# Scaling and adding a tile's first two gathered slots later, their product in fourth place, and row shifts of a weight one iteration later

## The chip, the core and the metric

The kernel runs on one core of one Trainium2 chip. The metric is the device time in microseconds (us). Before the change three runs gave 629.84, 631.80 and 633.22 us; the median is 631.8. A profile was taken of one more execution, and all times of single instructions come from it.

## What is computed

The inputs are x, 4096 rows of 512 numbers, and a 4096 x 4096 adjacency matrix with few nonzero entries in a row besides the diagonal. Two layers follow each other. The first is a graph convolution with a residual and a normalisation; the second is graph attention with a residual and a normalisation.

```python
a = adj + eye; d = sum(a, axis=1) ** -0.5
out = relu((d[:, None] * a * d[None, :] @ x) @ W.T + b)
x = layernorm(x + out)
...
scores = scores + 0.01 * eye - 1e16 * (1.0 - maximum(adj, eye))
x = layernorm(x + einsum('hqm,hmk,hko->qo', softmax(scores), v, Wo))
```

Entries of the adjacency matrix are below 1, so the mask term of -1e16 times (1 - adj) leaves the attention of each row on its own diagonal, where adj is replaced by at least 1. The attention of a row is then its own value vector, and the second layer is one product with a combined weight of Wv and Wo. The kernel uses this, and it tests at the end whether it may. Should the test fail, a general version (the function general) runs after it; with these inputs it does not.

## The kernel before

**Tiles.** The rows are cut into 32 tiles of 128 (NT = 32). The function few_edges_below_one does the work in two phases.

**First phase** (lines 1063 to 1108, about the first 217 us of the profile). Its loop runs over t from 0 to 32. In each iteration a tile of adj is loaded (a_t, kept for scanning, or a_n, which only passes through to be summed), ACT sums its rows or tests for negative entries (L710, L715), and for some tile j the product y = d * (x W^T) is made: rows of x turned by PE (L689), copied by ACT (L694), multiplied (L703), scaled by ACT (L736) and written to DRAM by POOL's queue. Between these steps a generator, second_weights (L617), builds the combined weight wvo: transposes ("t" steps), products ("p" steps), and at its end the step sums and centre. A "p" step begins on PE in one iteration and its end is called in the next through the variable left (L1090). The function centre takes the mean out of the weight's rows on DVE (L654), makes four row numbers (L658), and adds them to the weight on ACT (L660), four instructions in a row.

**Scanning.** DVE finds the entries of each row: for each of 8 segments of a tile it takes the 8 largest values and their places (L752, L753), then merges and sorts them in short instructions (L774, L783, L780). The generator steps holds this work and some(n) emits the next pieces of it, a fixed share in each step of either phase. match then moves the slots of a tile between rows in six stages, named KEY, ACROSS, RANKS, PERM, MOVE and END: a key made by ACT (L848), its transpose on PE (L855), ranks on ACT (L862), a permutation on DVE (L872), matmuls on PE (L881, L884), and copies and sums on DVE (L892 to L895). The result is, for every tile, nine slots: column numbers (cols_all) and weights (wr_all).

**Second phase** (lines 1112 to 1396). The loop runs over tiles i in an order of its own, and inside over steps k from 0 to 8. For each slot POOL gathers the 128 rows of y that it names, 256 KB, by an indirect DMA (gather, L1119), 18 slots ahead of use, into a pool of 19 buffers. ACT builds a 128 x 128 matrix for each slot (spread, L999), and PE multiplies matrix and gathered rows and adds up in zs[i] (L1337). Each product is two matmul instructions in the profile.

**Slots added ahead.** Some slots of a tile share one matrix. The list summed (L1116) says how many: 1 for tile 0, 2 for tiles 1 to 22, 5 (SAME) for tiles 23 to 31. presum(i, 0) scales the first slot on ACT in place (L1141); presum(i, k) adds a further slot times its weight on DVE (L1143). One product then serves them all; it uses matrix KH and slot 0. In the kernel before, presum of tile i+1 is called at the last steps of tile i: for two slots at k = 7 and k = 8. The product of the sum is the first of a tile (k = 0), and the other slots follow at k = 2 to 8.

**After the products.** One step into the next tile, scaled (L1194) and residual (L1202) on DVE make the first layer's row sums; PE turns the rows (L689) and multiplies them by wvo (L703); ACT and DVE normalise, and ACT's queue writes the result. load_own(i+2) at k = 2 loads two tiles through SP's queue (L1134, L550); reload (L993) loads tiles of adj again for scanning, through the same queue.

**What sets the order.** The instructions are emitted in program order, and a scheduler of the framework orders those of each engine by priority and by when it reckons them ready; keep_in_program_order pins an instruction. The framework also hands out the buffers and sets the semaphores. Each engine works its instructions off in the order so fixed.

Of the kernel before, what the change touches and what calls it, by code (L numbers as in the profile page):

```python
# [419 lines left out]
def few_edges_below_one(  # L420
# [18 lines left out]
    nc = tc.nc  # L439
    N, D = x.shape  # L440
    H, _, KD = wks.shape
    NT = N // P
# [10 lines left out]
    KH = 9  # L453
# [107 lines left out]
    def load_first(t, parts=1):  # L561
        if t in early or t in resident:
            return load_a(t, parts=2 if t == NT - 1 else parts)
        return load_a(t, pn, "a_n")
# [23 lines left out]
    def split_b():  # L588

        t = [p1.tile([P, D], FP, name="x_t", bufs=6)[:3] for _ in range(3)]  # L590
        nc.gpsimd.dma_start(t[0], bcast_rows(b0, D)[:3])
        for n in range(2):
            nc.vector.tensor_tensor(t[n + 1], t[n], t[n].bitcast(BF)[:, 1::2], ALU.subtract)
        for n in range(3):
            u, e = t[n].bitcast(BF)[:, 1::2], ident[:3, n : n + 1]
            if n == 0:
                nc.vector.tensor_scalar(b3, u, e, None, op0=ALU.mult)
            else:
                nc.vector.scalar_tensor_tensor(b3, u, e, b3, op0=ALU.mult, op1=ALU.add)

    def load_second_weights():

        nc.sync.dma_start(
            wv.rearrange("p (h f) -> p h f", h=H),
            wvs.rearrange("h (p j) k -> p h (j k)", j=ND),
        )
        su1 = p1.tile([P, 2, ND, D], FP, name="wo", bufs=1)
        nc.sync.dma_start(su1[:, 0], wo.rearrange("(r a) k o -> (a k) r o", a=2))
        return su1

    def order_second_weights():
        nc.gpsimd.tensor_copy(
            w_nat.rearrange("p j (h k) -> p j h k", h=H),
            wv.rearrange("p (h j k) -> p j h k", h=H, j=ND),
        )

    def second_weights(su1):  # L617

        wo_sb, wvT = su1[:, 0], su1[:, 1]

        def transposed(r):
            pt = ps_t.tile([P, 512], FP, name="pt")
            for j in range(ND):
                nc.tensor.transpose(pt[:, ts(j, P)], w_nat[:, j, ts(r, P)], ident)
            return pt

        def put(r, pt):
            nc.scalar.copy(
                wvT[:, r, :].rearrange("q (p j) -> q j p", j=ND),
                pt[:, :D].rearrange("q (j p) -> q j p", j=ND),  # L630
            )

        def product(dc):
            pa = ps_a.tile([P, D], FP, name="acc")
            for r in range(NP):
                nc.tensor.matmul(
                    pa, wvT[:, r, ts(dc, P)], wo_sb[:, r, :], start=(r == 0), stop=(r == NP - 1)
                )
            return pa

        def add(dc, pa):
            nc.scalar.copy(wvo[:, dc, :], pa)
            nc.gpsimd.tensor_tensor(wvo[:, dc, ts(dc, P)], wvo[:, dc, ts(dc, P)], ident, ALU.add)

        def sums():
            pa = ps_a.tile([P, D], FP, name="acc")
            for dc in range(ND):
                nc.tensor.matmul(pa, ones, wvo[:, dc, :], start=(dc == 0), stop=(dc == ND - 1))
            return pa

        def centre(pa):
            row = const.tile([P, ND], FP, name="row")
            for dc in range(ND):
                nc.vector.scalar_tensor_tensor(  # L654
                    wvo[:, dc, :], pa, -1.0 / D, wvo[:, dc, :], op0=ALU.mult, op1=ALU.add,
                    accum_out=row[:, dc : dc + 1],
                )
            nc.vector.tensor_scalar(row, row, -1.0 / D, None, op0=ALU.mult)  # L658
            for dc in range(ND):
                nc.scalar.activation(  # L660
                    wvo[:, dc, :], wvo[:, dc, :], AF.Identity, bias=row[:, dc : dc + 1]
                )

        for r in range(NP):
            yield "t", (lambda r=r: transposed(r)), (lambda pt, r=r: put(r, pt))
        for dc in range(ND):
            yield "p", (lambda dc=dc: product(dc)), (lambda pa, dc=dc: add(dc, pa))
        yield "p", sums, centre

    def load_keys():  # L670
        su2 = setup_tile()
        for n, w in ((0, wqs), (1, wks)):
            nc.sync.dma_start(
                su2[:, n].rearrange("p c d -> p (c d)"),
                w.rearrange("h (a d) k -> (h a) (d k)", a=P // H),
            )
        return su2
# [307 lines left out]
    def some(upto):  # L985
        while count[0] < upto:
            count[0] += 1
            next(work, None)
# [38 lines left out]
    def projected(t):  # L1027

        return t + 1 + sum(t >= e for e in SOONER)
# [30 lines left out]
        a_tiles[t] = load_first(t)  # L1060
    transpose_w()
    split_b()
    setup, left = iter(()), None
    for t in range(NT + 1):
        if t == 0:
            su1 = load_second_weights()
        if t + DEEP < NT:
            a_tiles[t + DEEP] = load_first(t + DEEP)
        if t == 3:
            order_second_weights()  # L1070
            setup = second_weights(su1)

        ahead = sum(at <= projected(t) for at, _ in due)
        turn = sum(at <= projected(t + (t >= LEAD)) for at, _ in due)
        turn_rows(turn, 3)
        kind, begin, end = next(setup, (None,) * 3) if ahead - done[1] < 2 else (None,) * 3
        got = begin() if kind == "t" else None
        if t < NT:
            if t in early:
                sum_negative(t, a_tiles[t])  # L1080
            else:
                sum_rows(deg_all[:, t : t + 1], a_tiles[t][:, : N // 2 if t == NT - 1 else N])
                more = None
                if t == NT - 1:
                    more = small.tile([P, 1], FP, name="more")
                    sum_rows(more, a_tiles[t][:, N // 2 :])
                scaling(t, more)
            if t in again:
                del a_tiles[t]
        if left:  # L1090
            left()
            left = None
        for j in [j for at, j in due if at == t]:
            keep_y(j, us.pop(j))
        while done[1] < ahead:
            j = due[done[1]][1]
            us[j] = times(evacuate(p1, "xT", turned.pop(j), t >= NT - 7), wT)
            done[1] += 1
        turn_rows(turn, 2)
        if kind == "t":  # L1100
            end(got)
        if kind == "p":
            left = lambda end=end, pa=begin(): end(pa)
        if t < NT - 5:
            match(*ALL)
        some((t + 1) * RATE)
# [6 lines left out]
    p2 = ctx.enter_context(tc.tile_pool(name="second", bufs=2))  # L1113
    AHEAD = 18

    summed = [1] + [2] * (NT - 1 - 9) + [SAME] * 9  # L1116
    slots = {}

# [18 lines left out]
    def presum(i, k):  # L1137
        g = slots[i * KH]
        w = wr_all[:, order[i], 1, k : k + 1]
        if k == 0:  # L1140
            nc.scalar.activation(g, g, AF.Copy, scale=w)  # L1141
            return
        nc.vector.scalar_tensor_tensor(  # L1143
            g, slots.pop(i * KH + k), w, g, op0=ALU.mult, op1=ALU.add
        )

    def last_products(ks, c):

# [128 lines left out]
    yo, zs, hs, pts, hTs, ws, sts, mats, halves = ({} for _ in range(9))  # L1277
# [28 lines left out]
    for i in range(NT + 2):  # L1306
# [6 lines left out]
        for k in range(KH):  # L1313
# [7 lines left out]
            if i == NT - 1:  # L1321

                if k == 4:
                    last_products((0, *range(SAME, KH)), HALVES[0])
                if k == 6:
                    scaled(i, HALVES[0])
                    residual(i, HALVES[0])
                    bias(i, HALVES[1])
                    last_products((0, *range(SAME, KH)), HALVES[1])
                if k == 7:  # L1330
                    pts[i] = transpose_rows(hs[i], (0, 1))
                    hTs[i] = p2.tile([P, ND, P], FP, name="hT", bufs=2)
                    tc.keep_in_program_order(nc.scalar.copy(
                        hTs[i][:, 0:2].rearrange("p c s -> p (c s)"), pts[i][:, : 2 * P]
                    ))
            elif i < NT and not 0 < k < summed[i]:
                nc.tensor.matmul(  # L1337
                    zs[i], mats[i][:, KH if k < summed[i] > 1 else k, :], slots.pop(i * KH + k),
                    start=False, stop=(k == KH - 1),
                )  # L1340
            if i < NT:
                gather(i * KH + k + AHEAD)
            build(1)
            if i + 1 < NT and k >= KH - summed[i + 1] and summed[i + 1] > 1:
                presum(i + 1, k - (KH - summed[i + 1]))
            if k == 1 and has_p and not ends:
                scaled(p)
# [74 lines left out]
```

## Time and profile before

| what | value |
|---|---|
| median of three runs | 631.8 us (629.84 to 633.22) |
| profiled execution, its own time | 632.17 us |
| its span, first to last instruction | 630.3 us |
| mean granted clock of PE | 0.946 |
| busy: PE, DVE, ACT, POOL | 523.2, 555.0, 497.7, 357.6 us |
| DMA, mean over the span | 345 GB/s |
| gathers on POOL | 288, 0.996 us each |
| products of the second phase (L1337) | 450 matmul instructions, 0.626 us each |
| additions of slots on DVE (L1143) | 58, 0.741 us each |
| scalings of slots on ACT (L1141) | 31, 0.713 us each |

Busy time counts an engine's instructions from start to end. Matmuls are pipelined, and their ends are modelled, so two matmuls that are listed with 0.6 us each may start 0.43 us apart. A wait in a listing stands in brackets after the instruction that waited, with its length and what ended it. "<-DVE g L1143" means that the engine was idle until DVE's instruction of line 1143, which writes tile g, had ended.

### The profile page before, as it was taken

To read this page: it belongs to the slowest core of one execution; us is meant where nothing else is said; L and a number is where in the kernel's file an instruction comes from. 1 tells how busy PE (TensorE), PEld (TensorE's weight loads), DVE (VectorE), ACT (ScalarE), POOL (GpSimd) and SP (SyncE) were. 2 spreads that over 40 slices of the span, in tenths; PEclk is the share of its full clock that TensorE was granted. 3 is DMA by queue.
4 is the path that set the end of the run, shared out by engine and by line. 5 is a ranking of instruction groups with operands and counts; after the bars stand their busy time and mean duration, and the time that the engine had idled before them with its cause. 6 is when DMAs were issued, how large, how long until landed. Compare 5 with 4: busy or idle time off the path is not lost. (4 is left out here: it accounts for less than half of the span.)

```text
span 630.3 us, 7782 instructions
## 1 busy us (share of the span) xinstructions
PE 523.2 (83%) x1537; PEld 241.2 (38%) x1537; DVE 555.0 (88%) x2037; ACT 497.7 (79%) x1093; POOL 357.6 (57%) x465
## 2 busy tenths in 40 slices
PE   1599886699968052799897999999999999989793
PEld 1344333345423021344443444444444444433251
DVE  5699999999999998799998999999999999854441
ACT  0859668688899858479978988998989899877751
POOL 5232323233323277677775667777777777777740
PEclk9999988999999566799998999999999999989898
DMA  8999999899999587999999999999999988888851
GB/s 327 401 420 423 421 427 428 332 416 426 425 425 424 238 282 226 354 383 397 398 397 399 402 368 327 389 354 381 313 394 366 317 265 280 280 276 244 286 163 38
DMA packets 57273, 217.68 MB, mean 345 GB/s; under 512 B 8701, under 2 KB 9981, under 8 KB 52864
## 3 DMA queue, kind: packets, MB, share of 16 engines
q1 hardware_dynamic: 23888, 115.48, 46.1%
q0 software_dynamic: 28192, 92.30, 41.7%
q10 hardware_dynamic: 5136, 9.31, 4.0%
q14 instruction: 43, 0.35, 0.2%
q8 instruction: 14, 0.23, 0.1%
HBM read 200.28 MB, written 16.78 MB: 344 GB/s over the span
## 5 line engine op out<-in xcount | busy, mean ns | idle before, releaser
L1124 POOL DMA_INDIRECT g<-y,cols_all x288 | 286.9, 996 | 101.9 <-issue 46.6
L1337 PE MATMUL acc<-g,s_t 128*128 128x512 f32 x450 | 221.6, 626 | 38.4 <-DVE g L1143 22.2
L752 DVE MAX8 v_all<-a_t 128x8 f32<-128x512 f32 x256 | 166.7, 678 | 15.9 <-DMA a_t<-in_adj_dram 15.9
L753 DVE FIND_INDEX8 idx<-v_all,a_t 128x8 uint32<-128x512 f32 x256 | 173.2, 684 | 0.0
L703 PE MATMUL acc<-wT,xT 128*128 128x512 f32 x256 | 121.8, 625 | 20.6 <-ACT xT L694 19.8
L1337 PEld LDWEIGHTS acc<-g,s_t 128*128 128x128 f32 x450 | 84.2, 199 | 133.0 <-issue 101.0
L703 PE MATMUL acc<-wvo,hT 128*128 128x512 f32 x256 | 117.8, 602 | 5.2 <-ACT hT L694 4.2
L715 ACT ACTIVATE dump<-a_t 128x2048 uint8<-128x2048 f32 (+1 forms) x50 | 119.2, 2383 | 0.0
L703 PEld LDWEIGHTS acc<-wT,xT 128*128 128x128 f32 x256 | 49.2, 200 | 78.1 <-issue 53.1
L703 PEld LDWEIGHTS acc<-wvo,hT 128*128 128x128 f32 x256 | 48.8, 193 | 66.9 <-issue 57.0
L1006 ACT ACTIVATE sq<-cols,wr_all 128x128 f32<-128x128 f32 x160 | 58.8, 393 | 6.7 <-DMA a_t<-in_adj_dram 6.1
L1143 DVE SCALAR_TENSOR_TENSOR g<-g,wr_all 128x512 f32<-128x512 f32 x58 | 43.0, 741 | 23.4 <-ACT s_t L1016 6.6
L1010 ACT ACTIVATE s_t<-sq,wr_all 128x128 f32<-128x128 f32 x128 | 58.5, 485 | 0.2
L722 POOL TENSOR_SCALAR deg<-deg_all 128x1 f32<-128x1 f32 x32 | 7.3, 229 | 78.5 <-DVE deg_all L970 45.5
L710 ACT ACTIVATE dump<-a_n 128x4096 uint8<-128x4096 f32 x13 | 47.3, 3639 | 0.0
L550 POOL DMA_DIRECT2D x_t<-in_x_dram x32 | 18.0, 565 | 41.6 <-PE pt L689 35.4
L783 DVE MAX8 top<-key 128x8 f32<-128x64 f32 x192 | 36.2, 213 | 0.1
L1141 ACT ACTIVATE g<-g,wr_all 128x512 f32<-128x512 f32 x31 | 22.1, 713 | 16.4 <-issue 10.0
L694 ACT COPY hT<-pt 128x512 f32<-128x512 f32 x31 | 18.0, 579 | 18.1 <-PE pt L689 17.9
L774 DVE SCALAR_TENSOR_TENSOR key<-key,top 128x64 f32<-128x64 f32 x128 | 32.2, 272 | 0.0
L694 ACT COPY xT<-pt 128x512 f32<-128x512 f32 x32 | 18.9, 600 | 14.3 <-PE pt L689 12.4
L1194 DVE SCALAR_TENSOR_TENSOR h<-yo,own_all,acc 128x512 f32<-128x512 f32 (+1 forms) x33 | 23.7, 719 | 5.1 <-PE acc L1337 2.6
(135 smaller groups left out, 661.4 us busy)
## 6 DMA issues: line engine op xcount, KB each, us to landing
a_t<-in_adj_dram SPq DMA_DIRECT2D x17, 2048.0 KB, 21.5
a_t<-in_adj_dram SPq DMA_DIRECT2D x56, 512.0 KB, 12.4
a_n<-in_adj_dram SPq DMA_DIRECT2D x13, 2048.0 KB, 15.8
x_t<-in_x_dram POOLq DMA_DIRECT2D x32, 256.0 KB, 11.3
yo<-y SPq DMA_DIRECT2D x32, 256.0 KB, 6.5
x_t<-in_x_dram SPq DMA_DIRECT2D x32, 256.0 KB, 7.3
out_dram<-r_t ACTq DMA_DIRECT2D x31, 256.0 KB, 6.1
y<-y_t POOLq DMA_DIRECT2D x18, 256.0 KB, 14.7
```

The lines of the kernel that those rows point to most:

```text
L694: copy = nc.scalar.copy(dst.rearrange("p c s -> p (c s)"), pt[:, :D])
L703: nc.tensor.matmul(u, srcT[:, dc, :], w[:, dc, :], start=(dc == 0), stop=(dc == ND - 1))
L710: nc.scalar.activation(dump[:, : part.shape[1]], part, AF.Copy, accum_out=dst)
L715: nc.scalar.activation(dump[:, o], a_t[:, o], AF.Relu, scale=-1.0, accum_out=neg_all[:, t, halves[0] : halves[0] + 1],)
L752: long.append(lambda o=o, seg=seg: nc.vector.max(v[:, o], seg))
L753: long.append(lambda o=o, seg=seg: nc.vector.max_index(idx[:, o], v[:, o], seg))
L783: return lambda: nc.vector.max(top[:, f, r * 8 : r * 8 + 8], keyf[:, f])
L1006: nc.scalar.activation(sq, cols1, AF.Square, bias=wr[:, 2, k : k + 1])
L1010: nc.scalar.activation(s_t[:, k, :], away(), AF.Relu, scale=wr[:, 3, k : k + 1], bias=wr[:, 1, k : k + 1],)
L1124: nc.gpsimd.indirect_dma_start(out=slots[j], out_offset=None, in_=y[:, :], in_offset=bass.IndirectOffsetOnAxis(ap=cols_all[:, t, k : k + 1 ...
L1143: nc.vector.scalar_tensor_tensor(g, slots.pop(i * KH + k), w, g, op0=ALU.mult, op1=ALU.add)
L1337: nc.tensor.matmul(zs[i], mats[i][:, KH if k < summed[i] > 1 else k, :], slots.pop(i * KH + k), start=False, stop=(k == KH - 1),)
```

## The change

Two things are moved. First, the four row shifts on ACT become a step of their own, of a kind "s", that the generator yields after "p" of sums. It has nothing to begin on PE, and its end, shift, is called at the left() of the iteration after centre's or a later one. The four instructions are pinned to program order. The variable row carries the four numbers from centre to shift.

Second, for tiles with two summed slots (1 to 22), the scaling on ACT is called at k = 8 of the tile before, not 7, and the addition on DVE at k = 1 of the tile itself, not at k = 8 of the one before. PE's products run in the order slot 2, 3, 4, then the sum at k = 3 (BASE), then slots 5, 6, 7, 8 at k = 4 to 7; k = 8 has none. Tile 0 and the tiles with five summed slots keep their order.

```diff
@@ second_weights
             nc.vector.tensor_scalar(row, row, -1.0 / D, None, op0=ALU.mult)
+            return row
+
+        def shift(row):
             for dc in range(ND):
-                nc.scalar.activation(
+                tc.keep_in_program_order(nc.scalar.activation(
                     wvo[:, dc, :], wvo[:, dc, :], AF.Identity, bias=row[:, dc : dc + 1]
-                )
+                ))
...
         yield "p", sums, centre
+        yield "s", None, shift
@@ loop of the first phase
-        if left:
-            left()
-            left = None
+        row = (left() if left else None) or row
+        left = None
...
+        if kind == "s":
+            left = lambda end=end, row=row: end(row)
@@ second phase
+    BASE = 3
...
+    def product(i, m, j, stop):
+
+        nc.tensor.matmul(zs[i], mats[i][:, m, :], slots.pop(j), start=False, stop=stop)
...
+            elif i < NT and summed[i] == 2:
+                if k == BASE:
+                    product(i, KH, i * KH, False)
+                else:
+                    m = k + 2 if k < BASE else k + 1
+                    if m < KH:
+                        product(i, m, i * KH + m, m == KH - 1)
             elif i < NT and not 0 < k < summed[i]:
-                nc.tensor.matmul(
-                    zs[i], mats[i][:, KH if k < summed[i] > 1 else k, :], slots.pop(i * KH + k),
-                    start=False, stop=(k == KH - 1),
-                )
+                product(i, KH if k < summed[i] > 1 else k, i * KH + k, k == KH - 1)
             if i < NT:
                 gather(i * KH + k + AHEAD)
             build(1)
-            if i + 1 < NT and k >= KH - summed[i + 1] and summed[i + 1] > 1:
+            if i + 1 < NT and summed[i + 1] == 2 and k == KH - 1:
+                presum(i + 1, 0)
+            if i < NT and summed[i] == 2 and k == 1:
+                presum(i, 1)
+            if i + 1 < NT and k >= KH - summed[i + 1] and summed[i + 1] > 2:
                 presum(i + 1, k - (KH - summed[i + 1]))
```

More of the change, by code (lines that the diff above doesn't have):

```diff
@@ L1062, in few_edges_below_one @@
     split_b()
-    setup, left = iter(()), None
+    setup, left, row = iter(()), None, None
     for t in range(NT + 1):
```

## The prediction

> **What bounds the kernel now.** I read the busy shares by slice first, then the waits, then the timelines of single engines. In the slices a digit 9 means 90% or more of 15.76 us.
>
> ```profile
> PE   1599886699968052799897999999999999989793
> ...
> DVE  5699999999999998799998999999999999854441
> ACT  0859668688899858479978988998989899877751
> ...
> PEclk9999988999999566799998999999999999989898
> DMA  8999999899999587999999999999999988888851
> ```
>
> DVE (VectorE) stands at 9 from the third slice to the thirty-fourth, but for three of them. The table by stage says the same in numbers:
>
> ```profile
> 390.00:540.00 150.00, 149.91 (x463) 67.98 (x462) 149.89 (x610) 137.96 (x404) 114.37 (x114) 1.00 0.95 336
> 540.00:606.00 66.00, 58.30 (x157) 25.07 (x156) 35.45 (x105) 48.87 (x138) 50.77 (x51) 0.95 0.85 271
> ```
>
> The columns are length, PE, weight load, DVE, ACT, POOL. From 390 to 540 us PE and DVE are both full. After 540 DVE has run out of scanning, and no engine is full. I then asked the timeline of DVE for its idle time between 30 us and the end of scanning (about 548 us). There are seven gaps above 0.3 us: 0.62 at 129.96 (ended by PE), 7.55 at 256.67, 0.47 at 276.41 (PE), 0.42 at 293.21 (ACT), 0.67 at 333.81 (ACT), 1.67 at 347.01 (PE) and 0.32 at 386.91 (its own result). That is 11.7 of 518 us. **VectorE's fixed work is the bound until 548 us**; whatever frees another engine counts only as far as it closes one of these gaps. The largest is seen here:
>
> ```profile
> 256.67 1.29 DVE L752 MAX8 v_all<-a_t 128x8 f32<-128x512 f32 x2 [7.55 <-DMA a_t<-in_adj_dram]
> ```
> ```profile
> 222.26 0.43 SPq L550 DMA_DIRECT2D x_t<-in_x_dram  x1
> 247.58 0.33 SPq L1134 DMA_DIRECT2D yo<-y  x1
> 248.85 0.33 SPq L550 DMA_DIRECT2D x_t<-in_x_dram  x1
> 249.23 4.16 SPq L545 DMA_DIRECT2D a_t<-in_adj_dram  x5
> ```
>
> The first reload of adjacency rows sits in SP's queue behind load_own(3), whose buffers come free with tile 0's scaled and residual on DVE (246.80 and 248.13). DVE starves on a load that DVE itself released late.
>
> PE's waits, the target of the edit:
>
> ```profile
> PE acc L1337 <- DVE g L1143: 22.2, 8, 11.0
> ```
> ```profile
> 248.27 10.18 PE L1337 MATMUL acc<-g,s_t 128*128 128x512 f32 x16 [10.96 <-DVE g L1143]
> ...
> 263.13 5.29 PE L1337 MATMUL acc<-g,s_t 128*128 128x512 f32 x6 [4.14 <-DVE g L1143]
> ```
>
> The eight waits are 10.96, 4.14 (tiles 1, 2), 1.62, 0.59, 0.94, 1.29 (tiles 6, 7, 8, 10), 1.02 and 1.67 (tiles 26, 27). The last two are five-slot tiles, which the edit leaves alone.
>
> After 548 us POOL is the quiet limit. Its gathers start every 1.25 us (0.95 and 0.30 between), so 288 take 360 us, and they run from 220.8 to 605 us. Nine take 11.25 us; PE's full tile takes 11.55 us, a five-slot tile some 9.2. In tiles 27 to 30 gathers land last: of PE's gaps, 1.67, 0.69 and 3.11 us end with a gather or with ACT work that stood behind one (ACT waited 2.50 us for the gather of tile 30).
>
> **What the Trainium skill says.** "TensorE: Matmul & The Clock Gate", section "What's actually happening", gives half clock after an idle window of about 3.4 us. The trace agrees: after the 10.96 us wait the first products start 1.7 to 1.9 us apart, later ones 0.86. The same page, "Architectural detail", calls ACT's and DVE's queues strict FIFO; so does the trace: ACT stands 4.01 us before the row shift while a sum of rows (L710) stands behind it. The Trainium skill's first page, "Trainium Kernel Development and Optimization", section "Key Constraints", says that DMAs from SP, ACT and POOL share the same 16 engines; the trace has them at 1.02 of full before the hole below, with several queues in use.
>
> **Part 1, row shifts later.** Removed from one place and added in a later one: four ACT instructions of about 0.71 us, 2.56 together. What goes is the wait ahead of them:
>
> ```profile
> 116.59 2.56 ACT L660 ACTIVATE wvo<-wvo,row 128x512 f32<-128x512 f32 x4 [4.01 <-DVE row L658]
> 119.06 0.67 ACT L736 ACTIVATE y_t<-acc,d_all 128x512 f32<-128x512 f32 x1
> 119.63 3.60 ACT L710 ACTIVATE dump<-a_n 128x4096 uint8<-128x4096 f32 x1
> ```
>
> That L710 frees the buffer of the next a_n load, which SP issues at 123.35, 18.4 us after the one before, where the next come 11.3 and 11.8 apart. The DMAs fall from 431 to 302 GB/s between 116 and 128 us: 129/431 of 12 us is 3.6 us of lost transfer. With the wait gone I expect the hole to close, and y, the gathers and tile 0 some 3.5 us earlier. But DVE has no gap there besides the 0.62, which comes from the same hold-up, and it reaches tile 1's work at 246.8 whatever starts early. **Worth 0.6 us**; 3.6 if DVE did not cover it.
>
> **Part 2, the order within a tile.** For tiles 1 to 22: 22 ACT scalings (0.71) and 22 DVE additions (0.74) are moved, not added; PE's eight products stay eight. No DMA is issued by a moved step. PE now does slots 2, 3, 4, then the sum, then 5 to 8. The sum is needed three products later, 3 x 0.86 = 2.58 us. The addition moves behind two steps of DVE, to just ahead of scaled; in the trace scaled follows the addition by 2.56 us at tile 2, 4.03 at tile 3, 0.65 at 5, and it is ahead of it by 0.65 to 2.08 at tiles 1, 6, 7, 8 and 10: there the addition already runs at its new place, and the whole 2.58 is margin. For 9 to 22 the new margin is old margin + 2.58 - distance: tile 9 0.98+2.58-1.32 = 2.2, 14 1.7, 18 0.95, 20 0.6. None is negative, so I expect no base wait there.
>
> *Tiles 1 and 2.* PE does three cold products (about 1.8 us each) inside the wait at tile 1; at tile 2 slot 5 can start near 266 rather than 269.35, because the addition ends at about 265. PE is 3.3 us ahead, and stays so until key transposes (L855) stop it at 311.96, 325.82 and 340.60 for ACT's key. The reload at 249.23 is not moved: scaled, addition and residual together end at the same time. Gain on DVE: the 0.47 gap at 276.41.
>
> *Tiles 6 to 10.* PE idles 7.48 us (the four waits above, 4.44, and 0.36, 0.37, 2.31 at L855). PE's recovery is worth only what DVE and ACT allow: the gaps 0.42, 0.67 and 1.67. ACT's key is now ahead of the scaling in its queue (0.71 sooner), so I take 2.5 of these 2.76.
>
> *What the edit costs.* The MOVE matmuls come after four products instead of three, 0.86 us later in the tile, and DVE's copy L892 waits for them. In the trace that copy starts 0.34 us after MOVE where it waits, 0.60 at tile 6, 0.75 at 9, 0.87 at 13. If PE is some 3 us ahead this is covered; I charge 0.5 us for tiles 12 to 14. The scaling comes one step nearer to its addition; the nearest today is 0.41 us at tile 5. Neither wait is seen in this form; bounds 0 and 3.7 us (rival S). A gain from less waiting cannot come twice, so not below nothing.
>
> *POOL.* Buffers come free in another order. At step 7 a gather now waits for a product issued ahead of the eight L703 matmuls (3.6 us), not behind them; I estimate one gather of 1.25 us more lead. POOL's waits over 0.4 us after 300 sum to 14.6. In the tail, 1.67+0.69+3.11 = 5.5 us of PE time stand behind gathers. If POOL is up to 1.5 us further ahead than DVE is, the tail gains 0 to 1.5; I take 0.7.
>
> **Sum.** 0.6 + 0.5 + 2.5 - 0.5 + 0.7 = 3.8 us. The profiled execution took 632.17 us, of which the span is 630.3 and 1.9 lie around it; it becomes 628.4. The median of the three runs, 631.8, is 0.4 below it: **628.0 us**.
>
> **Rivals.** *N, no change:* DVE and ACT keep their gaps, and PE's regained waits return as longer waits at L855. For it: 0.05 us between key and transpose at tiles 5, 9 to 12 of the matching. Against: gaps ended by PE. Gain 0.6 to 1; 631. *S, slower:* PE is not ahead when it reaches MOVE, since the scheduler places the additions later still, and DVE waits in L892 at tiles 6 to 14: 0.86 minus today's margin is 0.60+0.86+0.86+0.45+0.21+0.24+0.33+0.11 = 3.7 us; 635.5. It decides once the base product still waits a microsecond or more at tiles 6 to 10. Against it: the additions are at the new place already. *B, more:* the 3.5 us of Part 1 reach the end after all, because DVE's order lets tile 0's scaled come sooner and so the reload at 249.23: 3.8 + 3.5 gives 624.5. Against: DVE is full until 249. That the sum's code changes nothing in order can't be: the products' order on PE is written out.
>
> **How the numbers follow.** Forecast 0.42 (626.5 to 629.7), N 0.20, S 0.18, B 0.20. About 0.5%, 3.2 us, is what a measurement of this kernel tells from no change: below 628.6 lies B and two thirds of the forecast, 0.47; above 635.0 most of S, 0.16; between them 0.37. The range 624.0 to 634.5 leaves out the lower part of B and most of S.
>
> **What would show it.** Right: no wait of L1337 for the addition over 0.5 us at tiles 3 to 22; the DMA hole at 116 to 128 closed; the 7.55 us gap of DVE still there, others shrunk; scanning over near 545. Wrong: L892 or the addition waiting on DVE (S); DVE's big gap shrunk or shifted by 3 us (B); unchanged end of scanning (N).

## The result and the profile after

Twenty executions of each kernel: **627.75 us** after (625.09 to 631.92) and 630.85 us before (626.50 to 633.43). The ratio is 0.9952, its 95% interval 0.9934 to 0.9969: the change takes off 3.1 us, 0.5%. On two of the four chips used further below the executions of one kernel spread over more than 2%; medians there are of all executions, while ratios and intervals leave out those over 1.5% above the fastest of their kernel. The profiled execution of the changed kernel took 629.12 us, with a span of 627.2. Its lines stand some lines lower in the code: L1155 is the product (L1337 before), L1149 the addition (L1143), L1147 the scaling, L663 the row shift, L1204 scaled, L1130 the gather.

The busy shares by slice (15.7 us each), TensorE's granted clock and the transfers, from the page of the kernel after:

```profile
DVE  5699999999999998799999999999999999844441
...
PEclk9899988979979768899999999999999999998997
...
GB/s 326 403 418 425 422 424 424 432 421 396 423 427 423 181 271 219 370 392 398 399 397 398 400 396 366 384 359 393 312 379 358 312 264 274 253 282 263 282 180 39
```

VectorE's row is as full as before. The eighth slice, which stood at 332 GB/s, is at 432, but the tenth, which stood at 426, is at 396. In PEclk the digit 8 of the twenty-second slice (331 to 347 us) has become a 9; this stretch comes back below. The stages of before, asked again:

```profile
390.00:540.00 150.00, 147.97 (x453) 66.60 (x454) 149.82 (x607) 136.06 (x403) 113.91 (x112) 1.00 0.94 332
540.00:604.00 64.00, 55.80 (x161) 24.82 (x159) 33.22 (x108) 48.09 (x133) 49.07 (x50) 0.97 0.85 269
```

**First phase.** Timelines of ScalarE, then of GpSimd:

```profile
120.97 2.57 ACT L663 ACTIVATE wvo<-wvo,row 128x512 f32<-128x512 f32 x4
...
137.79 0.69 ACT L740 ACTIVATE y_t<-acc,d_all 128x512 f32<-128x512 f32 x1 [4.46 <-POOL d_all L729]
```
```profile
135.56 0.46 POOL L726 TENSOR_SCALAR deg<-deg_all 128x1 f32<-128x1 f32 x2 [8.15 <-DVE deg_all L974]
```

The row shift stands without a wait. But 17 us later ScalarE waits 4.46 us for the degree of a tile, which GpSimd makes from a sum of VectorE (L974), and GpSimd had waited 8.15 us for that. The wait has moved, and a smaller hole in the transfers has come with it. The first gather starts at 221.68 us, against 220.77 before.

**Start of the second phase.** Timelines of SP and of VectorE:

```profile
247.12 0.33 SPq L1140 DMA_DIRECT2D yo<-y  x1
247.94 0.33 SPq L550 DMA_DIRECT2D x_t<-in_x_dram  x1
248.33 2.50 SPq L545 DMA_DIRECT2D a_t<-in_adj_dram  x4
```
```profile
254.91 0.75 DVE L1204 SCALAR_TENSOR_TENSOR h<-yo,own_all,acc 128x512 f32<-128x512 f32 x1 [6.12 <-PE acc L1155]
255.94 1.29 DVE L756 MAX8 v_all<-a_t 128x8 f32<-128x512 f32 x2 [0.29 <-DMA a_t<-in_adj_dram]
```

The reload still stands behind own rows. VectorE's gap is 6.12 + 0.29 us in place of 7.55, and tile 1 is scaled in it, which before came at 264.91.

**Waits for the addition.** The total, from the waits, and the three in tiles 6 to 8, from TensorE's timeline:

```profile
PE acc L1155 <- DVE g L1149: 17.4, 12, 5.5
```
```profile
312.00 1.13 PE L1155 MATMUL acc<-g,s_t 128*128 128x512 f32 x2 [1.59 <-DVE g L1149]
325.21 1.12 PE L1155 MATMUL acc<-g,s_t 128*128 128x512 f32 x2 [1.35 <-DVE g L1149]
...
339.13 1.13 PE L1155 MATMUL acc<-g,s_t 128*128 128x512 f32 x2 [1.45 <-DVE g L1149]
```

Tile 1's wait is 5.45 us, half of 10.96. After 270 us, however, there are ten waits with 11.1 us together, against six with 7.1 before. The last search of a maximum (MAX8) starts at 529.7 us (532.4 before), the last gather at 603.6 (606.0).

### The profile page after: what moved, and what is told of

Its sections match the earlier page's. It is cut to its first block, busy times and chain, and to the rows that moved or that the text cites. A ratio compares the mean times of both kernels' runs of the same rounds, so it can differ in the third digit from the quotient of the medians.

```text
span 627.2 us, 7808 instructions
## 1 busy us (share of the span) xinstructions
PE 523.3 (83%) x1537; PEld 239.4 (38%) x1537; DVE 555.0 (88%) x2037; ACT 496.3 (79%) x1093; POOL 358.5 (57%) x465
## 5 line engine op out<-in xcount | busy, mean ns | idle before, releaser
L1130 POOL DMA_INDIRECT g<-y,cols_all x288 | 288.0, 1000 | 97.4 <-issue 39.5
L1155 PE MATMUL acc<-g,s_t 128*128 128x512 f32 x450 | 220.4, 617 | 36.1 <-DVE g L1149 17.4
L707 PE MATMUL acc<-wT,xT 128*128 128x512 f32 x256 | 123.8, 634 | 15.4 <-ACT xT L698 15.3
L1155 PEld LDWEIGHTS acc<-g,s_t 128*128 128x128 f32 x450 | 80.9, 194 | 128.7 <-issue 68.3
L1149 DVE SCALAR_TENSOR_TENSOR g<-g,wr_all 128x512 f32<-128x512 f32 x58 | 43.1, 743 | 27.1 <-ACT g L1147 10.6
L1147 ACT ACTIVATE g<-g,wr_all 128x512 f32<-128x512 f32 x31 | 22.1, 714 | 19.2 <-DMA g<-y,cols_all 15.1
L1204 DVE SCALAR_TENSOR_TENSOR h<-yo,own_all,acc 128x512 f32<-128x512 f32 (+1 forms) x33 | 23.8, 722 | 11.5 <-PE acc L1155 9.1
```

The source lines that it names most:

```text
L707: nc.tensor.matmul(u, srcT[:, dc, :], w[:, dc, :], start=(dc == 0), stop=(dc == ND - 1))
L1130: nc.gpsimd.indirect_dma_start(out=slots[j], out_offset=None, in_=y[:, :], in_offset=bass.IndirectOffsetOnAxis(ap=cols_all[:, t, k : k + 1 ...
L1149: nc.vector.scalar_tensor_tensor(g, slots.pop(i * KH + k), w, g, op0=ALU.mult, op1=ALU.add)
L1155: nc.tensor.matmul(zs[i], mats[i][:, m, :], slots.pop(j), start=False, stop=stop)
```

## The experiments

Theories. **D**, the prediction's: VectorE's work and its gaps set the time until 548 us. **P**: TensorE's work does. **G**: the 288 gathers do, by their cadence and the slots they wait for. **B**: what Part 1 frees in the first phase reaches the end. The series ran on four chips. On two of them the kernel before took 631.5 and 631.6 us, on the other two 701.6 and 698.5; ratios are always to the kernel before on the same chip. The changed kernel itself was not run again beside these.

### Each part alone

Part 1 alone is the kernel before with the diff's first two hunks; Part 2 alone has only the third.

> Part 1 alone: the row shifts one iteration later, the order of products and additions as before. Theory D (VectorE's fixed work and its gaps set the end, in the first phase too): ACT's 4.01 us wait and the hole in the transfers at 116 to 128 us go, VectorE's gap of 0.62 us goes, and a later wait for VectorE takes the rest back: 630.3 to 630.9 us against 630.9, at most 0.6 less. Theory B (the 3.5 us that ScalarE and the transfers gain reach the end): 627.3 us.

> Part 2 alone: the sum fourth and its scaling and addition later, the row shifts as before. Theory D: nearly the whole of the measured 3.1 us, 627.8 to 628.4 us, with VectorE's gaps after 240 us as in the changed kernel. Theory B: 630.9 us, nothing.

Measured: 700.90 against 701.63 us (ratio 1.0034, interval 1.0006 to 1.0063) and 710.83 (1.0176, 1.0124 to 1.0227). Neither number was expected by any theory, since the kernel before itself took 11% more. For Part 1 alone the medians and the ratio point opposite ways, so no difference is shown there. Both were measured again on other chips.

> Part 1 alone again. Part 2 alone measured 0.9977 (630.0 against 631.5), both parts 0.9952, so the difference leaves some 1.6 us for Part 1. Theory A (the parts add up: Part 1 saves 1.5 us by itself): 629.3 to 629.8 us beside a kernel before at 631. Theory D (VectorE's scanning bounds the first phase, Part 1 is worth 0 to 0.6 alone): 630.4 to 631.

> Part 2 alone again, because the first series took 701.6 us for the kernel before, 11% over its time until then. Theory D (VectorE's fixed work and its gaps set the end; Part 1 is worth 0 to 0.6): where the kernel before takes about 631 us, 627.8 to 628.4. Theory B (Part 1's 3.5 us of transfers reach the end): 630.9. Where the kernel before takes about 700 us, 705 to 712 as in the first series.

Measured: Part 1 alone 631.08 against 631.58 us (0.9988, 0.9968 to 1.0007); Part 2 alone 630.01 against 631.53 (0.9977, 0.9957 to 0.9998). B falls: Part 1 by itself is at most 2.0 us, and not distinct from nothing. Its trace shows the same move as after: tenth slice 389 GB/s, and ScalarE waits 4.06 us at 137.94. Part 2 saves 0.1 to 2.7 us. The middles add up to 2.2 us, both together measured 3.1 (2.0 to 4.2); that the parts help each other isn't shown.

### TensorE's order alone

The kernel after with the row shifts of before and, in the second phase:

```diff
-            if i + 1 < NT and summed[i + 1] == 2 and k == KH - 1:
-                presum(i + 1, 0)
-            if i < NT and summed[i] == 2 and k == 1:
-                presum(i, 1)
-            if i + 1 < NT and k >= KH - summed[i + 1] and summed[i + 1] > 2:
+            if i + 1 < NT and k >= KH - summed[i + 1] and summed[i + 1] > 1:
```

> Of Part 2 only TensorE's order: the sum's product fourth, but its scaling and addition where they stood (slots 6 and 7 of the tile before); row shifts as before. If what counts is that TensorE multiplies three slots of a tile before it needs the sum, the gain is that of the whole Part 2, 627.8 to 628.4 us. If what counts is that VectorE makes the addition later, behind the scaled and residual of the tile before, it stays at 630.5 to 631 us.

Measured: 704.83 against 701.63 us (1.0057, 1.0019 to 1.0095), on the chip where Part 2 whole gave 1.0176. There the moved products alone made the kernel slower, and the moved scaling and addition slower still. For the other chips it says nothing, and which half of Part 2 gains there stays open.

### Own rows out of the reload's way

```diff
-            if k == 2:
+            if k == 2 and i + 2 not in (3, 4):
+                load_own(i + 2)
+            if k == 8 and i + 2 in (3, 4):
                 load_own(i + 2)
```

The two loads are pinned to program order, and so are the first reloaded tile's searches ahead of tile 1's scaled.

> The changed kernel with one more edit: SP issues the first reloaded tile's four transfers ahead of the own rows of tile 3 (which wait for VectorE's residual of tile 0), and VectorE scans that tile before it scales tile 1. Theory D (any microsecond in which VectorE stands still before 548 us is lost, and the 6.1 us gap at 249 to 255 us is the largest one): the gap falls to 1 to 3 us and the time to 624 to 626 us. Rival: the transfers wait for the buffer's release anyway, or TensorE and the gathers hold the later part, and it stays at 627.3 to 628.3 us.

Measured: 706.44 against 701.63 us (1.0142, 1.009 to 1.0194), on the same chip. The four reload transfers were issued at 243.83 us, ahead of tile 3's own rows at 270.96. VectorE, though, stood in a dozen waits of 1.0 to 4.7 us between 240 and 268 us, ahead of small operations that don't wait in the profiles of before and after, so the question of what its gap is worth was not answered.

### More work on VectorE and on TensorE

The results of the spare operations are not used. First for VectorE, where the operation's input is a weight in the first kernel and h of the tile before in the second:

```diff
+            if i < NT and summed[i] == 2 and k == 5:
+                spare = p2.tile([P, D // 2], FP, name="spare", bufs=1)
+                nc.vector.tensor_scalar(spare, wvo[:, 0, : D // 2], 1.0, None, op0=ALU.mult)
```

> The changed kernel with one spare VectorE operation on 128x256 numbers (some 0.4 us by the durations of VectorE's 128x512 operations, 0.75 us, halved) in each of tiles 1 to 22, 22 of them, some 9 us of VectorE's time. Theory D: nearly all of it reaches the end, 634 to 637 us. Theory P (TensorE sets the pace of tiles 3 to 22): VectorE has room, 628 to 630. Theory G (the row gathers set the pace): 628 to 631.

> The changed kernel with one spare VectorE operation (128x256, 0.30 us in the run before, in which all 22 had slid into VectorE's gap at 244 to 255 us), now made dependent on h so that one falls into each of 21 tiles: 6.3 us of VectorE's time spread over 270 to 510 us. Theory D (VectorE's fixed work sets the end): 5 to 6 us more than the changed kernel, about 633 to 634. Theory P (TensorE sets the pace there, VectorE follows): 0 to 2 us more, 628 to 630.

Measured: 630.94 against 631.53 us (0.9987, 0.9966 to 1.0007), with all 22 operations in VectorE's gap at 244 to 255 us; and spread over the tiles 627.79 against 631.58 (0.9938, 0.9911 to 0.9965). The group of the spread operations, count and busy time after the shapes:

```profile
L1364 DVE TENSOR_SCALAR spare<-h 128x256 f32<-128x256 f32 x22 | 6.8, 309 | 0.0
```

6.8 us more of VectorE's work, and the ratio is not above the changed kernel's 0.9952. **D falls**: its 5 to 6 us would need the changed kernel to stand at about 0.985 on this chip. The last MAX8 now starts at 539.6 us, 9.9 later, and no gather waits as much as 0.6 us for its column numbers. The same operations pushed into one place measured some 3 us more than spread (0.9987 against 0.9938). The two ran on different chips, so it is only a reading that VectorE's work counts by what it stands in front of.

TensorE:

```diff
+            if summed[i] == 2:
+                nc.tensor.matmul(zs[i], ones3, b3, start=True, stop=True)
             bias(i, HALVES[0] if i == NT - 1 else slice(0, D))
```

> The changed kernel with the bias product (3x512, 0.385 us) made twice in each of tiles 1 to 22: 22 more, 8.5 us of TensorE's time at most. Theory P (TensorE is busy without a gap at 380 to 500 us and paces the gathers by the slots that it frees): 4 to 8 us more than the changed kernel, 632 to 636. Theory D: the waits for the addition shrink in its place, 0 to 2 more, 628 to 630. Theory G (the gathers' own 1.25 us cadence): 0 to 1.

Measured: 626.17 against 631.58 us (0.9918, 0.9882 to 0.9955).

```profile
L1320 PE MATMUL acc<-b,ones 3*128 3x512 bf16 x22 | 8.6, 393 | 3.8 <-ACT wo L740 3.8
```

8.6 us more of TensorE's work brought no rise either; the ratio is even below the changed kernel's 0.9952, which the intervals don't separate. **P falls** as well. After 270 us its waits for the addition are 6.0 us, against 11.1 after, so the extra products seem to fill waits.

### Gather slots and GpSimd

The first kernel has 21 slots and fetches its own rows later, the second has 18 slots (bufs=AHEAD), the third one GpSimd operation more per tile.

```diff
-        slots[j] = p2.tile([P, D], FP, name="g", bufs=AHEAD + 1)
+        slots[j] = p2.tile([P, D], FP, name="g", bufs=AHEAD + 3)
...
-            if k == 2:
-                load_own(i + 2)
+            if k == 2 and i:
+                load_own(i + 1)
```

> The changed kernel with 21 gather slots in place of 19 (same order of gathers, 18 ahead); to make room, the own rows y and x of a tile have two buffers in place of three and are fetched one tile later. Theory G (the end is set by the chain of 288 gathers: first one at 221 to 226 us, 1.25 us each, plus what they wait for slots that TensorE and VectorE free late; that excess was 25.9 us before, 22.6 after): the excess falls by 3 to 8 us, the time to 620 to 625 us. Theory D or P (VectorE or TensorE sets the end): 627 to 628.5, since neither has less to do.

> The changed kernel with 18 gather slots in place of 19, nothing else. Theory G: each gather's slot must be free one product earlier, and the excess of the gathers grows by 1 to 5 us: 629 to 633 us. Theory D or P: 627 to 628.5.

> The changed kernel with one spare GpSimd operation (h times 1 on 128x256) among the gathers of each of 21 tiles. No trace shows its duration on GpSimd; by VectorE's 0.3 us for the same and GpSimd's 0.227 us for 128x1 it is at least 0.3 us, so 6 us or more of GpSimd's time in all. Theory G: nearly all of it reaches the end, 633 us or more, in the proportion of its measured duration. Theory D or P: GpSimd is busy 57% of the time and has room, 627 to 629.

Measured, against 698.48 us: 708.90 (1.0117, 1.0029 to 1.0204), 702.89 (1.0051, 1.0019 to 1.0082) and 703.97 (1.0114, 1.0076 to 1.0152). The spare operation took 0.957 us on GpSimd:

```profile
L1364 POOL TENSOR_SCALAR spare<-h 128x256 f32<-128x256 f32 x22 | 21.0, 957 | 3.0 <-DVE h L1212 2.6
```

All three ran where the kernel before takes 698 us, and all that follows is for that chip. With 21.0 us more on GpSimd the time is no more than 10.6 us above that of the kernel before. The traces say why: between the gathers GpSimd waits 77.7 us with 18 slots, 78.6 with 21, and 58.0 with the spare work (counted beyond the 0.30 us that pass between any two gathers). The spare work went into waits, so GpSimd's own time was not the limit there, and the number of slots was hardly felt. On the chips of 631 us these waits are 6.5 to 11.9 us in all, so nothing follows for them; no run there changes the gathers, but their traces speak on **G**, as the next part shows.

### What the seven traces have in common

Seven kernels have a trace from the chips where the kernel before takes 631 us. Excess is the time from the first to the last gather less 287 times 1.252 us. The next column is the time from tile 8's bias product to tile 9's; the one after it, when TensorE was at half clock between 275 and 540 us.

| kernel | ratio | excess, us | tile 8, us | half clock from |
|---|---|---|---|---|
| before | 1 | 25.9 | 16.9 | 343.2 |
| Part 1 alone | 0.9988 | 24.6 | 15.6 | 313.9 and 341.3 |
| VectorE's work in one place | 0.9987 | 25.3 | 15.6 | 344.1 |
| Part 2 alone | 0.9977 | 23.3 | 15.5 | 344.3 |
| after | 0.9952 | 22.6 | 13.9 | none |
| VectorE's work spread | 0.9938 | 21.1 | 13.5 | none |
| TensorE's work more | 0.9918 | 21.2 | 13.8 | none |

Three stretches of 3.4 us of the kernel before, from the table by stage (length, TensorE, weight load, VectorE, ScalarE, GpSimd, granted clock):

```profile
336.40:339.80 3.40, 1.89 (x5) 0.47 (x3) 3.31 (x24) 3.40 (x11) 2.66 (x3) 1.00 1.04 401
339.80:343.20 3.40, 1.67 (x7) 1.01 (x8) 3.40 (x12) 3.40 (x7) 0.86 (x2) 1.00 1.02 395
343.20:346.60 3.40, 3.40 (x5) 1.16 (x4) 2.14 (x9) 1.52 (x5) 2.29 (x3) 0.50 1.03 401
```

In the second TensorE is busy for 1.67 of 3.40 us; in the third its clock is 0.50. Its timeline there, and GpSimd's a little later:

```profile
340.60 0.32 PE L855 MATMUL pt<-ident,rank_key 128*128 128x128 f32 x1 [2.31 <-ACT rank_key L848]
...
342.30 4.54 PE L1337 MATMUL acc<-g,s_t 128*128 128x512 f32 x6 [0.94 <-DVE g L1143]
```
```profile
353.34 0.94 POOL L1124 DMA_INDIRECT g<-y,cols_all  x1 [2.65 <-PE acc L1337]
```

Two waits stand close together, 2.31 and 0.94 us, and half clock follows; six matmuls then take 4.54 us, and a gather waits 2.65 us for the slot. In the kernel after the waits of this tile are 0.40 and 1.45 us, and the clock stays:

```profile
337.50:340.90 3.40, 1.95 (x11) 0.96 (x10) 3.31 (x12) 3.30 (x6) 2.49 (x4) 1.00 1.02 393
340.90:344.30 3.40, 3.40 (x10) 1.49 (x9) 3.40 (x16) 0.71 (x3) 2.70 (x3) 1.00 1.03 398
```

With such a stretch tile 8 takes 15.5 us or more, without one 13.5 to 13.9: at least 1.6 us. The three kernels without one are the three with the lowest ratios. This does not carry the whole gain, though. Part 2 alone has the stretch, and its excess is already 2.6 us below before, 0.7 above after. From tile 3's bias product to tile 11's it takes 100.2 us with the stretch, where after takes 102.3 without one and before 103.0. Nor do the traced executions follow the ratios: VectorE's work spread, with no stretch, took 631.17 us (its first gather came at 226.2), Part 2 alone, with one, 628.91. Where the windows lie can differ from execution to execution as well, and no run changed the clock alone. The missing stretch is a possible part of the gain, not a shown cause.

GpSimd's waits fit all seven. In each trace the next gather starts no sooner than 0.30 us after the last has ended. What GpSimd waits beyond that, in waits above 0.33 us from the first gather to the last, is 11.9, 10.3, 10.7, 9.2, 7.4, 6.5 and 6.8 us, in the order of the table; the other 14 to 15 us of the excess lie in gathers that themselves took longer. The last such wait ends at 493 us or earlier. From there to the last gather the gathers follow each other without a further wait, as at the end of after:

```profile
600.91 0.95 POOL L1130 DMA_INDIRECT g<-y,cols_all  x1 [0.30 <-issue]
602.17 1.15 POOL L1130 DMA_INDIRECT g<-y,cols_all  x1 [0.31 <-issue]
603.62 0.95 POOL L1130 DMA_INDIRECT g<-y,cols_all  x1 [0.30 <-PE pt L693]
```

What follows the last gather takes 22.8 to 25.6 us in all seven. So on these chips the gathers set the pace from there on, for 107 us or more, and the change counts by what it takes off their waits ahead of that. **G** is what the traces support; an experiment on these chips is missing.

## Why the number was right and the reasons were not

**The bound.** "VectorE's fixed work is the bound until 548 us" is the step that failed. VectorE is full, but full with work that is done ahead of need. The trace of before could have told it. Asked for the tile of column numbers, which VectorE's whole scanning ends in, it answers who waited for the instruction that writes it (L895):

```profile
who waited for it (us, times):
  POOL g L1124: 0.3, 1
```

That is one of the 0.30 us that pass between any two gathers; in every tile the columns were there at least 5.9 us ahead of the first gather that uses them. So closing VectorE's gaps need not be worth their length, and 6.8 us more of its work brought no rise.

**Part 1, 0.6.** Measured alone 0.8, from 2.0 faster to 0.4 slower: right within what can be told. The hole at 116 to 128 us closed, as forecast. "The gathers and tile 0 some 3.5 us earlier" was wrong: the first gather came 0.9 us later after, 0.6 later with Part 1 alone. Most of the time was given back at 137 us, in a wait for a degree whose sum stands in VectorE's queue; that sum had moved by 0.7 us only, from 135.99 to 135.26. That half of the argument, that VectorE sets the pace here, held. Why the last row sums on ScalarE then came 4.6 us later, at 189.58 us, was not traced.

**Part 2.** Its terms made 3.2 us (0.5 + 2.5 - 0.5 + 0.7); alone it measured 1.5 (0.1 to 2.7), so they were too large together.
- *0.5 for the gap at 276.41:* it is gone, but no measure of time, by the bound's failure.
- *2.5 of the gaps 0.42, 0.67 and 1.67:* after has 1.22 at 345.65 and 0.73 at 357.44 instead, 2.0 in place of 2.8. The same holds.
- *"No base wait there":* wrong, 1.59, 1.35 and 1.45 us at tiles 6 to 8, and ten in all after 270 us. The prediction had the addition at its new place there already, just behind scaled. It starts 3.4, 4.2 and 4.6 us behind scaled in after, where it was 1.4, 0.7 and 2.1 before, and that uses up the margin of 2.58 us. That TensorE, freed from tile 1's wait, starts tile 3 at 271.7 us in place of 276.4 is not needed for it: Part 2 alone starts it at 276.8 and waits 0.70, 1.34 and 1.94 us there.
- *-0.5 for the copy behind MOVE:* no VectorE gap over 0.3 us stands ahead of L896. The charge should have been nothing.
- *0.7 in the tail:* the last gather is 2.4 us earlier, but the tail has its own waits, and nothing separates this term.

**Rival S** was to decide once the sum still waits a microsecond or more at tiles 6 to 10. It did wait, and the time fell: the wait of the copy, from which S had its 3.7 us, did not come, and the sum's wait doesn't tell of it. **B** fell; of **N**, that regained waits come back elsewhere is what the traces show, at the addition and not at the transposes.

So the 628.0 beside 627.75 is a sum of wrong terms, and its closeness is luck: 3.8 us were forecast from a median of 631.8, and 3.1 measured from one of 630.85. What fits the runs in its place: up to 493 us gathers wait now and then, often for a slot that TensorE frees late, and neither VectorE nor TensorE is itself short of time; from there on the gathers run at their own pace. The change took GpSimd's waits from 11.9 to 7.4 us in the two traces. The difference arises at 335 to 354 us, where they are 6.8 us before and 1.3 after, and the missing half-clock stretch may be a part of it. This is read from traces and not shown by an experiment: on these chips no run changed the gathers or the clock alone.

## What to carry to other kernels

An engine at 90% or more is only the bound if someone waits for what it makes: ask the trace for the last tile that it writes and for who waited for it. Ask also which engine works without a wait up to the end; here it was GpSimd, which the page shows busy for 57% of the span, as it counts the 0.30 us between gathers as idle. Test a bound by adding work to it, spread as the real work is; two such runs spoke against the reading here. When waits of TensorE are moved, look at how they fall together within some 3.4 us, not only at their sum.

## What the runs showed of the hardware

**Half clock after a half-busy window.** In the seven traces 14 stretches of clock 0.5 begin between 270 and 600 us, in steps of 3.4 us. Each follows a window of 3.41 us in which TensorE was busy, by its modelled ends, for 0.52 of it or less. No window at full clock with 0.54 or more was followed by one; at 0.49 to 0.53 both occur. The Trainium skill ("TensorE: Matmul & The Clock Gate", section "HAM oscillation — how this bites in real kernels") gives as the rule that no idle gaps over about 3.4 us should occur. Here single waits of 1.6 to 2.1 us were enough; the measurement decides, and the prediction, which took the rule as it stands, did not look for it.

**Chips that differ.** On two of the four chips the unchanged kernel took 11% more. Each chip was used once, so the chip and the moment can't be told apart. In a trace from there (Part 1 alone, first run), half clock came back every 27 to 31 us from 304 to 482 us, and VectorE stood ahead of small operations. The same group there and, under its old line, in the kernel before on its own chip:

```profile
L784 DVE TENSOR_SCALAR rec<-rec,row1n 128x24 f32<-128x24 f32 x32 | 7.9, 263 | 10.7 <-issue 6.0 <-DVE rec L784 2.6 <-DVE rec L829 1.2
```
```profile
L780 DVE TENSOR_SCALAR rec<-rec,row1n 128x24 f32<-128x24 f32 x32 | 6.9, 260 | 0.0
```

Between 240 and 256 us VectorE has six such waits of 1.2 to 3.9 us, four of them near one, two or three times the gathers' 1.25 us, while gathers follow each other without a pause. The Trainium skill ("SBUF — State Buffer", section "SBUF: two separate sides") says that some VectorE operations and GpSimd's exclude each other at a shared pair of ports; that fits, but why it shows on two chips and not on the others stays open. Part 2, a gain of 1.5 us on one chip, was a loss of 9.2 us on such a one; the runs don't show why.
